# Attention with the keys on partitions: scores transposed, exp without a maximum, row sums by a product with ones

## The chip, the core and the metric

The kernel runs on one core of one Trainium2 chip. The metric is the device time of one execution in microseconds (us); the kernel before takes 4026.67 us, the median of 3 runs (4023.98 to 4026.76). All data are fp32.

## The reference

A block of an image network: group norm, attention over the 1024 pixels with 4 heads, a projection and a residual. `x` is [16, 512, 32, 32], so 16 batches of 512 channels by n = 1024 pixels.

```python
xg = x.reshape(b, NUM_GROUPS, -1)                       # 8 groups of 64 channels
mu = jnp.mean(xg, axis=-1, keepdims=True)
var = jnp.var(xg, axis=-1, keepdims=True)
xn = ((xg - mu) * jax.lax.rsqrt(var + EPS)).reshape(b, c, h, w)
xn = xn * norm_gamma[:, None, None] + norm_beta[:, None, None]
qkv = jnp.einsum('oc,bchw->bohw', qkv_w, xn) + qkv_b[:, None, None]
q, k, v = jnp.split(qkv, 3, axis=1)                     # each to [b, 4 heads, n, 128]
attn = jax.nn.softmax(jnp.einsum('bhnd,bhmd->bhnm', q, k) * scale, axis=-1)
out = jnp.einsum('bhnm,bhmd->bhnd', attn, v)
out = jnp.einsum('oc,bchw->bohw', proj_w, out) + proj_b[:, None, None]
return x + out
```

Inputs and weights are random normal, the weights scaled so that q and k have a variance of about one; gamma is ones, beta and all biases are zeros (the kernel does not use that).

## The kernel before

Everything is laid out with channels on the 128 partitions, in four chunks of a batch, and pixels along the free axis. A head has 128 channels. The main loop runs over **steps** `s`: 16 batches x 4 heads x 8 blocks of 128 queries = 512 steps.

A step has five parts. `scores(s)` (L208) multiplies a block of 128 queries with all 1024 keys of the head, two products of 512 columns into one tile of two PSUM banks, with queries on partitions and keys along the free axis. VectorE takes the row's maximum (L213), ScalarE (ACT) the exponential with the maximum as its bias and the row's sum as a by-product (L216). `weights` (L221, L222) takes the reciprocal of the 128 sums, one element per partition, and scales the block with it. `transposes` (L232) turns the block on TensorE (PE), 8 transposes of 128x128 into PSUM, and VectorE (L235) and ACT (L237) copy four of them each to SBUF. After every four steps `weighted_sum` (L247) multiplies the 512 turned queries with v, 8 products of 512 columns, and ACT adds v's bias (L253).

Beside the steps run **units**, products that later heads need. `qk_unit` (L163) makes half of q or k of the next head, 4 products of 512 columns; q goes out through VectorE (L169), k through ACT (L171). `v_unit` (L177, L182) makes v of all heads for one block of 128 keys. `proj_unit` (L187, L192) makes the projection of the batch before and adds bias and residual, and SyncE stores it. `plan_head` lays them on the eight steps of a head with `spread`; the statistics and the normalisation (L146) of the next batch lie on heads 2 and 3. All these units, the small products of the group norm and the outputs of `weighted_sum` share the PSUM pool `ps_a` of two buffers.

The order of work on each engine comes from the program's text and from the scheduler of the tile framework, which moves instructions by its own estimate of when they can start. Each engine then takes its instructions strictly in that order, waiting on semaphores of other engines. At the start, 48 products (L103) of the weights with beta make a bias for q, k and v, since beta is not added to the normalised input.

## Time and profile before

| | us |
|---|---|
| median of 3 runs | 4026.67 (4023.98 to 4026.76) |
| profiled execution, span | 4023.7 |
| TensorE busy | 3996.6 (99%) |
| VectorE (DVE) busy | 1716.4 (43%) |
| ScalarE (ACT) busy | 1150.7 (29%) |
| GpSimd (POOL) busy | 16.8 |

The span runs from the first to the last instruction of the profiled execution. In the rows, PE is TensorE's matmuls and PEld its weight loads. A row of a group names the line, the engine, the operation, output and inputs, the shape and the number of instructions; behind the bar stand the busy time, the mean of one in ns, and the idle time of the engine just before them with what ended it. A timeline row begins with start and length in us. The profile counts two records for each fp32 product, and one for each transpose. "L135 PE pv" is the second product of the group norm, and L177's `pv` is v.

### The profile page before, as it was taken

Reading aid. Unit: us, or ns where it says so; the run is one execution under the profiler, and the core shown is the slowest. Engines: PE = TensorE matmul, PEld = TensorE weight load, DVE = VectorE, ACT = ScalarE, POOL = GpSimd, SP = SyncE. Lnnn points to the kernel's source line nnn. Section 1 sums busy time; section 2 is a strip of 40 time slices with the busy share of each in tenths; the row PEclk is TensorE's granted clock in tenths of the full one; section 3 lists DMA queues with packets and bytes.
Section 4 is the critical chain, followed back from the end, with each engine's and each line's share of the span. In section 5 each row is a group of like instructions: output and inputs, shape, how many; then the busy total and the mean of one; then the engine's idle time right before and its main releaser. Section 6 shows DMA issues by size and latency. Waiting matters only on the chain.

```text
span 4023.7 us, 30686 instructions
## 1 busy us (share of the span) xinstructions
PE 3996.6 (99%) x12448; PEld 2009.3 (50%) x12448; DVE 1716.4 (43%) x2688; ACT 1150.7 (29%) x1921; POOL 16.8 (0%) x22
## 2 busy tenths in 40 slices
PE   7999999999999999999999999999999999999999
PEld 4544545445454454544545455454544545545454
DVE  2434434344343443434435344453434434345343
ACT  1332323323232232322323223232222322323222
POOL 0000000000000000000000000000000000000000
PEclk9999999999999999999999999999999999999999
DMA  2001000010100101001010010100001000010000
GB/s 84 0 1 42 1 29 14 0 42 1 34 8 0 42 0 42 0 1 42 0 42 0 3 40 1 42 0 11 32 1 42 1 17 26 0 42 1 11 11 21
DMA packets 29517, 73.28 MB, mean 18 GB/s; under 512 B 3776, under 2 KB 3776, under 8 KB 29376
## 3 DMA queue, kind: packets, MB, share of 16 engines
q1 hardware_dynamic: 27648, 67.12, 4.8%
q10 hardware_dynamic: 1728, 4.21, 0.3%
q8 instruction: 97, 1.59, 0.2%
q14 instruction: 44, 0.36, 0.0%
HBM read 37.76 MB, written 33.55 MB: 18 GB/s over the span
## 4 chain that ended last, share of the span: by engine, by line
PE 99%; DMA 0%; DVE 0%; ACTq 0%; issue 0%; POOL 0%; ACT 0%
PE pqk L163 22%; PE po L247 22%; PE s L208 22%; PE t L232 11%; PE pp L187 11%; PE pv L177 11%; PE pb L103 0%; DMA x<-in_x 0%; DMA wqkv<-in_qkv_wT 0%; PE pv L135 0%; PE pm L124 0%; ACTq L86 0%; DVE pt L235 0%; POOL rstd L139 0%; DVE xn L146 0%
## 5 line engine op out<-in xcount | busy, mean ns | idle before, releaser
L208 PE MATMUL s<-qk,qk 128*128 128x512 f32 x2048 | 965.9, 593 | 0.0
L163 PE MATMUL pqk<-xn,wqkv 128*128 128x512 f32 x2048 | 918.2, 594 | 2.4 <-DVE xn L146 2.4
L247 PE MATMUL po<-pt,v 128*128 128x512 f32 x2048 | 901.3, 593 | 0.3 <-DVE pt L235 0.3
L213 DVE TENSOR_REDUCE nmax<-s 128x1 f32<-128x1024 f32 x512 | 623.1, 1217 | 484.0 <-PE s L208 483.4
L235 DVE COPY pt<-t 128x512 f32<-128x512 f32 x512 | 351.3, 686 | 1052.5 <-PE t L232 1052.5
L216 ACT ACTIVATE p<-s,nmax 128x1024 f32<-128x1024 f32 x512 | 571.2, 1116 | 600.9 <-DVE nmax L213 600.7
L163 PEld LDWEIGHTS pqk<-xn,wqkv 128*128 128x128 f32 x2048 | 390.1, 191 | 493.5 <-issue 486.5
L247 PEld LDWEIGHTS po<-pt,v 128*128 128x128 f32 x2048 | 387.7, 190 | 482.6 <-issue 465.7
L232 PEld LDWEIGHTS t<-ident,p 128*128 128x128 f32 x4096 | 479.2, 141 | 264.3 <-issue 240.7
L232 PE MATMUL t<-ident,p 128*128 128x128 f32 x4096 | 531.7, 273 | 2.0 <-DVE p L222 1.3
L237 ACT COPY pt<-t 128x512 f32<-128x512 f32 x512 | 299.8, 586 | 639.0 <-PE t L232 638.6
L208 PEld LDWEIGHTS s<-qk,qk 128*128 128x128 f32 x2048 | 349.4, 190 | 246.2 <-issue 246.2
L177 PE MATMUL pv<-wqkv,xn 128*128 128x512 f32 x1024 | 449.4, 592 | 0.0
L187 PE MATMUL pp<-o,wproj 128*128 128x512 f32 x1024 | 449.4, 592 | 0.0
L222 DVE TENSOR_SCALAR p<-p,rinv 128x1024 f32<-128x1024 f32 x512 | 383.7, 749 | 10.1
L253 ACT ACTIVATE o<-po,bias 128x512 f32<-128x512 f32 x128 | 87.9, 687 | 952.4 <-PE po L247 952.4
L187 PEld LDWEIGHTS pp<-o,wproj 128*128 128x128 f32 x1024 | 194.6, 190 | 244.9 <-issue 239.4
L177 PEld LDWEIGHTS pv<-wqkv,xn 128*128 128x128 f32 x1024 | 194.6, 190 | 244.9 <-issue 230.6
L221 DVE RECIPROCAL rinv<-total 128x1 f32<-128x1 f32 x512 | 83.4, 163 | 398.5 <-ACT p L216 396.1
L171 ACT ACTIVATE qk<-pqk,bias 128x512 f32<-128x512 f32 x128 | 88.0, 687 | 374.7 <-PE pqk L163 374.7
L192 DVE SCALAR_TENSOR_TENSOR y<-pp,projb_sb,x 128x512 f32<-128x512 f32 x128 | 95.8, 749 | 165.0 <-PE pp L187 164.8
L182 ACT COPY v<-pv 128x512 f32<-128x512 f32 x128 | 74.9, 585 | 248.1 <-PE pv L177 248.1
(30 smaller groups left out, 443.6 us busy)
## 6 DMA issues: line engine op xcount, KB each, us to landing
x<-in_x SPq DMA_DIRECT2D x64, 512.0 KB, 3.6
out_y<-y SPq DMA_DIRECT2D x128, 256.0 KB, 2.2
wqkv<-in_qkv_wT ACTq DMA_DIRECT2D x4, 768.0 KB, 8.5
wproj<-in_proj_wT ACTq DMA_DIRECT2D x4, 256.0 KB, 8.2
gamma_sb<-in_gamma ACTq DMA_DIRECT2D x1, 2.0 KB, 3.8
beta_sb<-in_beta ACTq DMA_DIRECT2D x1, 2.0 KB, 4.7
qkvb_sb<-in_qkv_b ACTq DMA_DIRECT2D x1, 6.0 KB, 5.9
projb_sb<-in_proj_b ACTq DMA_DIRECT2D x1, 2.0 KB, 5.6
```

The lines of the kernel that those rows point to most:

```text
L163: nc.tensor.matmul(acc, wqkv[c][:, ts(o, P)], xns[b, c][:, ts(half, HALF)], start=(c == 0), stop=(c == NCC - 1),)
L177: nc.tensor.matmul(acc[:, :C], xns[b, c][:, ts(j, P)], wqkv[c][:, 2 * C : 3 * C], start=(c == 0), stop=(c == NCC - 1),)
L187: nc.tensor.matmul(acc, wproj[c][:, ts(o, P)], os_[b, c][:, ts(half, HALF)], start=(c == 0), stop=(c == NCC - 1),)
L192: nc.vector.scalar_tensor_tensor(y, acc, projb_sb[:, o : o + 1], xs[b, o][:, ts(half, HALF)], ALU.add, ALU.add)
L208: nc.tensor.matmul(sc[:, ts(half, HALF)], qs[b, h][:, ts(qb, P)], ks[b, h][:, ts(half, HALF)], start=True, stop=True,)
L213: nc.vector.tensor_reduce(nmax, sc, AX.X, ALU.max, negate=True)
L216: nc.scalar.activation(p, sc, AF.Exp, bias=nmax, accum_out=total)
L222: nc.vector.tensor_scalar_mul(ps[s], ps[s], rinv)
L232: nc.tensor.transpose(pt[:, i, :], p[:, ts(4 * g + i, P)], ident)
L235: nc.vector.tensor_copy(dst, pt)
L237: nc.scalar.copy(dst, pt)
L247: nc.tensor.matmul(acc, vs[b, j][:, ts(h, P)], pt[:, j, :], start=(j == 0), stop=(j == NB - 1),)
```

## The change

**Scores.** The operands of the products change places: the block of a step is now 128 keys on partitions, and the 1024 queries lie along the free axis. ACT takes the exponential straight from PSUM, with the factor 1/sqrt(128) as its scale, without a maximum and without the sum. The result has the keys on partitions, which is the form that the product with v needs: the maxima, `weights` and `transposes` with their copies are gone.

**Sums.** VectorE adds the eight blocks of a head into `tot` (L255, L257). At the head's end `denominators` multiplies `tot` with a matrix of ones (L264), two products of 512 columns in `ps_a`; each partition then has all sums. VectorE takes their reciprocals, 128x512 each (L266), and one instruction (L269) takes the larger of a sum and its reciprocal and adds these along the row into a column of `spans`.

**Output.** `weighted_sum` now follows each step: two products of 512 columns (L280) add into `po`, a tile of two PSUM banks that lives for a whole head, in a pool `ps_o` with one buffer. At the head's end VectorE multiplies it with the reciprocals (L288).

**Biases and beta.** The products with beta at the start are gone. Beta is added to the normalised input (L72), on VectorE for batch 0, on GpSimd for the others. The scale leaves q, and both q and k go out through ACT (L208). v's bias is added as v leaves PSUM, on VectorE (L221).

**General branch.** At the end the sums in `spans` are added and compared with 1e20. If they are larger or not a number, `flag` is 1, and the branch `general_path` does all batches again with the maximum, the sums and the transposes, in a loop over batches. It stands in the program, and each engine loads the flag and branches.

```diff
+    def apply(self, xn, x, mu, sc, c, eng):
+        self.nc.vector.tensor_scalar(
+            xn, x, mu[:, c : c + 1], sc[:, c : c + 1], ALU.subtract, ALU.mult
+        )
+        eng.tensor_scalar(xn, xn, self.beta[:, c : c + 1], None, ALU.add)
...
+    redo = nc.values_load(flag[0:1, 0:1], min_val=0, max_val=1,
...
+    with tc.If(redo > 0):
+        with ExitStack() as general:
+            general_path(
...
     ppool = ctx.enter_context(tc.tile_pool(name="p", bufs=4))
-    ptpool = ctx.enter_context(tc.tile_pool(name="pt", bufs=2))
+    lpool = ctx.enter_context(tc.tile_pool(name="l", bufs=2))
     ypool = ctx.enter_context(tc.tile_pool(name="y", bufs=3))
-    small = ctx.enter_context(tc.tile_pool(name="small", bufs=6))
     gn = ctx.enter_context(tc.tile_pool(name="gn", bufs=2))
     ps_s = ctx.enter_context(tc.tile_pool(name="ps_s", bufs=2, space=bass.MemoryType.PSUM))
-    ps_t = ctx.enter_context(tc.tile_pool(name="ps_t", bufs=2, space=bass.MemoryType.PSUM))
+    ps_o = ctx.enter_context(tc.tile_pool(name="ps_o", bufs=1, space=bass.MemoryType.PSUM))
     ps_a = ctx.enter_context(tc.tile_pool(name="ps_a", bufs=2, space=bass.MemoryType.PSUM))
...
-    # beta goes through the qkv product as a bias: W (xhat * gamma) + (W beta + b)
-    bias = const.tile([P, NOC], F32, name="bias")
-    for o in range(NOC):
-        pb = ps_a.tile([P, HALF], F32, tag="acc", name=f"pb_{o}")
-        for c in range(NCC):
-            nc.tensor.matmul(
-                pb[:, 0:1], wqkv[c][:, ts(o, P)], beta_sb[:, c : c + 1],
-                start=(c == 0), stop=(c == NCC - 1),
-            )
-        nc.vector.tensor_add(bias[:, o : o + 1], pb[:, 0:1], qkvb_sb[:, o : o + 1])
...
     def normalise(b, c):
-        xn = xnpool.tile([P, N], F32, tag="xn", name=f"xn_{b}_{c}")
-        nc.vector.tensor_scalar(
-            xn, xs[b, c], mus[b][:, c : c + 1], scs[b][:, c : c + 1],
-            ALU.subtract, ALU.mult,
-        )
-        xns[b, c] = xn
+        xns[b, c] = xnpool.tile([P, N], F32, tag="xn", name=f"xn_{b}_{c}")
+        norm.apply(xns[b, c], xs[b, c], *scaled[b], c, nc.vector if b == 0 else nc.gpsimd)
...
-        dst = store[b, h][:, ts(half, HALF)]
-        if which == 0:
-            nc.vector.tensor_scalar(dst, acc, bias[:, o : o + 1], SCALE, ALU.add, ALU.mult)
-        else:
-            nc.scalar.activation(dst, acc, AF.Identity, bias=bias[:, o : o + 1])
+        nc.scalar.activation(
+            store[b, h][:, ts(half, HALF)], acc, AF.Identity, bias=qkb_sb[:, o : o + 1]
+        )
...
         vs[b, j] = vpool.tile([P, C], F32, tag="v", name=f"v_{b}_{j}")
-        nc.scalar.copy(vs[b, j], acc[:, :C])
+        nc.vector.tensor_add(vs[b, j], acc[:, :C], vb_sb)
...
-    # ---- attention, one block of 128 queries of a head at a time ----
-    ps, sums, pts = {}, {}, {}
+    ps, tot, po, rinv = {}, {}, {}, {}
     def where(s):
-        bh, qb = divmod(s, NB)
-        return (*divmod(bh, HEADS), qb)
+        bh, j = divmod(s, NB)
+        return (*divmod(bh, HEADS), j)
     def scores(s):
-        b, h, qb = where(s)
+        b, h, j = where(s)
         sc = ps_s.tile([P, N], F32, tag="s", name=f"s_{s}")
         for half in range(NH2):
             nc.tensor.matmul(
-                sc[:, ts(half, HALF)], qs[b, h][:, ts(qb, P)], ks[b, h][:, ts(half, HALF)],
+                sc[:, ts(half, HALF)], ks[b, h][:, ts(j, P)], qs[b, h][:, ts(half, HALF)],
                 start=True, stop=True,
             )
-        nmax = small.tile([P, 1], F32, tag="nmax", name=f"nmax_{s}")
-        nc.vector.tensor_reduce(nmax, sc, AX.X, ALU.max, negate=True)
-        p = ppool.tile([P, N], F32, tag="p", name=f"p_{s}")
-        total = small.tile([P, 1], F32, tag="total", name=f"total_{s}")
-        nc.scalar.activation(p, sc, AF.Exp, bias=nmax, accum_out=total)
-        ps[s], sums[s] = p, total
-    def weights(s):
-        rinv = small.tile([P, 1], F32, tag="rinv", name=f"rinv_{s}")
-        nc.vector.reciprocal(rinv, sums.pop(s))
-        nc.vector.tensor_scalar_mul(ps[s], ps[s], rinv)
-    def transposes(s):
+        ps[s] = ppool.tile([P, N], F32, tag="p", name=f"p_{s}")
+        nc.scalar.activation(ps[s], sc, AF.Exp, scale=SCALE)
+        if j == 1:
+            tot[b, h] = lpool.tile([P, N], F32, tag="tot", name=f"tot_{b}_{h}")
+            nc.vector.tensor_add(tot[b, h], ps[s - 1], ps[s])
+        elif j > 1:
+            nc.vector.tensor_add(tot[b, h], tot[b, h], ps[s])
+    def denominators(b, h):
+        t = tot.pop((b, h))
+        for half in range(NH2):
+            l = ps_a.tile([P, HALF], F32, tag="acc", name=f"l_{b}_{h}_{half}")
+            nc.tensor.matmul(l, ones, t[:, ts(half, HALF)], start=True, stop=True)
+            r = lpool.tile([P, HALF], F32, tag=f"rinv{half}", name=f"rinv_{b}_{h}_{half}")
+            nc.vector.reciprocal(r, l)
+            worst = lpool.tile([P, HALF], F32, tag="worst", name=f"worst_{b}_{h}_{half}")
+            i = (b * HEADS + h) * NH2 + half
+            nc.vector.scalar_tensor_tensor(
+                worst, l, 1.0, r, ALU.mult, ALU.max, accum_out=spans[:, i : i + 1]
+            )
+            rinv[b, h, half] = r
+    def weighted_sum(s):
+        b, h, j = where(s)
         p = ps.pop(s)
-        chunk, qi = divmod(s, QPH)
-        if qi == 0:
-            pts[chunk] = ptpool.tile([P, NB, HALF], F32, tag="pt", name=f"pt_{chunk}")
-        for g in range(NB // 4):
-            pt = ps_t.tile([P, 4, P], F32, tag="t", name=f"t_{s}_{g}")
-            for i in range(4):
-                nc.tensor.transpose(pt[:, i, :], p[:, ts(4 * g + i, P)], ident)
-            dst = pts[chunk][:, 4 * g : 4 * g + 4, ts(qi, P)]
-            if g % 2 == 0:
-                nc.vector.tensor_copy(dst, pt)
-            else:
-                nc.scalar.copy(dst, pt)
-    def weighted_sum(chunk):
-        b, h, qb = where(chunk * QPH)
-        half = qb // QPH
-        pt = pts.pop(chunk)
-        if half == 0:
+        if j == 0:
+            po[b, h] = ps_o.tile([P, N], F32, tag="o", name=f"po_{b}_{h}")
+        for half in range(NH2):
+            nc.tensor.matmul(
+                po[b, h][:, ts(half, HALF)], vs[b, j][:, ts(h, P)], p[:, ts(half, HALF)],
+                start=(j == 0), stop=(j == NB - 1),
+            )
+        if j == NB - 1:
+            o = po.pop((b, h))
             os_[b, h] = opool.tile([P, N], F32, tag="o", name=f"o_{b}_{h}")
-        acc = ps_a.tile([P, HALF], F32, tag="acc", name=f"po_{chunk}")
-        for j in range(NB):
-            nc.tensor.matmul(
-                acc, vs[b, j][:, ts(h, P)], pt[:, j, :],
-                start=(j == 0), stop=(j == NB - 1),
-            )
-        # a row of the softmax sums to one, so v's bias is added to the sum
-        o = 2 * HEADS + h
-        nc.scalar.activation(
-            os_[b, h][:, ts(half, HALF)], acc, AF.Identity, bias=bias[:, o : o + 1]
-        )
+            for half in range(NH2):
+                nc.vector.tensor_mul(
+                    os_[b, h][:, ts(half, HALF)], o[:, ts(half, HALF)], rinv.pop((b, h, half))
+                )
...
-                spread(plan, proj_units(b - 1), 3, 7)
+                spread(plan, proj_units(b - 1), 2, 7)
...
     steps = B * HEADS * NB
     plan = []
-    for s in range(steps + 3):
+    for s in range(steps + 1):
         if s < steps:
-            b, h, qb = where(s)
-            if qb == 0:
+            b, h, j = where(s)
+            if j == 0:
                 plan = plan_head(b, h)
             scores(s)
-            for u in plan[qb]:
+            for u in plan[j]:
                 u()
-        if 1 <= s <= steps:
-            weights(s - 1)
-        if s >= 3 and (s - 3) % QPH == QPH - 1:
-            weighted_sum((s - 3) // QPH)
-        if 2 <= s < steps + 2:
-            transposes(s - 2)
+        if s > 0:
+            if s % NB == 0:
+                denominators(*where(s - 1)[:2])
+            weighted_sum(s - 1)
+    total = gn.tile([P, 1], F32, tag="total", name="total")
+    nc.vector.tensor_reduce(total, spans, AX.X, ALU.add)
+    fine = gn.tile([P, 1], F32, tag="fine", name="fine")
+    nc.vector.tensor_scalar(fine, total, LIMIT, None, ALU.is_le)
+    nc.vector.tensor_scalar(flag, fine, -1.0, 1.0, ALU.mult, ALU.add)
     for u in proj_units(B - 1):
         u()
```

The change also moves instructions. On TensorE, where a head (here the third of batch 0) follows another, these rows stood before; `t` are the transposes, `s` the scores, `pqk` a unit:

```order
L208 MATMUL s_754<-qk_0_1_427,qk_0_1_348 128x512 x2
L232 MATMUL t_0_765<-ident,p_695 128x128 x4
L232 MATMUL t_1_771<-ident,p_695 128x128 x4
L208 MATMUL s_777<-qk_0_2_668,qk_0_2_552 128x512 x2
L163 MATMUL pqk_3_0_0_786<-xn_0_250,wqkv_124 128x512
L163 MATMUL pqk_3_0_0_786<-xn_1_252,wqkv_126 128x512
L163 MATMUL pqk_3_0_0_786<-xn_2_254,wqkv_128 128x512
L163 MATMUL pqk_3_0_0_786<-xn_3_256,wqkv_130 128x512
L232 MATMUL t_0_795<-ident,p_718 128x128 x4
L232 MATMUL t_1_801<-ident,p_718 128x128 x4
```

Nothing ties the two heads together there. At the same place of the changed kernel, behind the unit `pqk_3_0_0`, TensorE has these; `l` are the sums, `po_1` is the old head's output and `po_2` the new head's:

```order
L264 MATMUL l_1_0_484<-tot_1_400,ones 128x512
L264 MATMUL l_1_1_490<-tot_1_400,ones 128x512
L280 MATMUL po_1_402<-p_467,v_7_267 128x512 x2
L247 MATMUL s_501<-qk_0_2_371,qk_0_2_433 128x512 x2
L247 MATMUL s_511<-qk_0_2_371,qk_0_2_433 128x512 x2
L247 MATMUL s_530<-qk_0_2_371,qk_0_2_433 128x512 x2
L204 MATMUL pqk_3_0_1_517<-xn_0_175,wqkv_66 128x512
L204 MATMUL pqk_3_0_1_517<-xn_1_178,wqkv_67 128x512
L280 MATMUL po_2_508<-p_475,v_0_218 128x512 x2
```

Three score tiles and half a unit now lie between the sums and the new head's first output product `po_2`, which waits for VectorE. VectorE has at that place:

```order
L257 TENSOR_TENSOR tot_1_400<-tot_1_400,p_467 128x1024
L266 RECIPROCAL rinv_1_0_486<-l_1_0_484 128x512
L266 RECIPROCAL rinv_1_1_492<-l_1_1_490 128x512
L269 SCALAR_TENSOR_TENSOR worst_1_0_488,spans<-l_1_0_484,rinv_1_0_486 128x512
L269 SCALAR_TENSOR_TENSOR worst_1_1_494,spans<-l_1_1_490,rinv_1_1_492 128x512
L288 TENSOR_TENSOR o_1_498<-po_1_402,rinv_1_0_486 128x512
L288 TENSOR_TENSOR o_1_498<-po_1_402,rinv_1_1_492 128x512
L255 TENSOR_TENSOR tot_2_506<-p_475,p_504 128x1024
```

The two products that empty `po_1` (L288) stand behind both reciprocals and both L269. From head 2 to head 3 of a batch the last `tot` addition stands behind the next batch's four normalisations:

```order
L64 TENSOR_TENSOR sc<-rstd,gamma_sb 128x4
L69 TENSOR_SCALAR xn_0_620<-x_0_356,mu,sc 128x1024
L69 TENSOR_SCALAR xn_1_623<-x_1_358,mu,sc 128x1024
L69 TENSOR_SCALAR xn_2_650<-x_2_360,mu,sc 128x1024
L69 TENSOR_SCALAR xn_3_653<-x_3_362,mu,sc 128x1024
L257 TENSOR_TENSOR tot_2_506<-tot_2_506,p_610 128x1024
L266 RECIPROCAL rinv_2_0_628<-l_2_0_626 128x512
```

In the program's text the normalisations belong to head 3; here they have moved ahead of the end of head 2's sum.

More of the change, by code (lines that the diff above doesn't have):

```diff
@@ L6 @@
 from concourse import mybir
-from concourse.bass import ts
+from concourse.bass import ds, ts
 from concourse.masks import make_identity
@@ L14 @@
 AX = mybir.AxisListType
+P = 128
 HEADS = 4
@@ L70, in attention_block @@
     load_x(0)
-    ident = const.tile([P, P], F32, name="ident")
-    make_identity(nc, ident)
-    avg = const.tile([P, P], F32, name="avg")
     nc.vector.memset(avg, 0.0)
@@ L114, in stats_chunk @@
             mvs[b] = gn.tile([P, NCC, 2], F32, tag="mv", name=f"mv_{b}")
[L115 to L118 removed]
+        norm.chunk(mvs[b], xs[b, c], c)
     def stats_group(b):
[L121 to L150 removed]
+        scaled[b] = norm.group(mvs.pop(b))
+    def normalise(b, c):
+        xns[b, c] = xnpool.tile([P, N], F32, tag="xn", name=f"xn_{b}_{c}")
+        norm.apply(xns[b, c], xs[b, c], *scaled[b], c, nc.vector if b == 0 else nc.gpsimd)
     def qk_unit(b, h, which, half):
```

211 lines of the change are left out of this document (162 added, 49 removed).

## Prediction

> **What bounds the kernel now.** I read the page first: the busy table, the slices and the chain of waits.
>
> ```profile
> span 4023.7 us, 30686 instructions
> PE 3996.6 (99%) x12448; PEld 2009.3 (50%) x12448; DVE 1716.4 (43%) x2688; ACT 1150.7 (29%) x1921; POOL 16.8 (0%) x22
> PE   7999999999999999999999999999999999999999
> PEclk9999999999999999999999999999999999999999
> PE pqk L163 22%; PE po L247 22%; PE s L208 22%; PE t L232 11%; PE pp L187 11%; PE pv L177 11%; PE pb L103 0%; DMA x<-in_x 0%; DMA wqkv<-in_qkv_wT 0%; PE pv L135 0%; PE pm L124 0%; ACTq L86 0%; DVE pt L235 0%; POOL rstd L139 0%; DVE xn L146 0%
> ```
>
> TensorE works in every slice but the first, at the full granted clock, and 99% of the chain is its own matmuls. DVE and ACT are under half full. So a matmul taken away is worth its whole slot, and anything that makes TensorE wait costs its whole length. A busy time cannot price a slot, since matmuls overlap (the transposes' 531.7 us would be 13% of the span; the chain gives them 11%). The slots come from the starts in the timeline of TensorE, in the middle of the run:
>
> ```profile
> 1007.66 1.04 PE L232 MATMUL t<-ident,p 128*128 128x128 f32 x8
> 1008.53 1.88 PE L208 MATMUL s<-qk,qk 128*128 128x512 f32 x4
> 1010.25 7.03 PE L177 MATMUL pv<-wqkv,xn 128*128 128x512 f32 x16
> 1017.12 1.04 PE L232 MATMUL t<-ident,p 128*128 128x128 f32 x8
> ```
>
> Eight transposes take 1008.53 - 1007.66 = 0.87 us (0.109 each); 16 records of 512 columns take 1017.12 - 1010.25 = 6.87 us (0.429 each). The profile counts two records per fp32 product, so a product is 0.86 us, and a `scores` or a pair of `po` products is 1.72.
>
> **Removed and added on TensorE.** The groups by line:
>
> ```profile
> L232 PE MATMUL t<-ident,p 128*128 128x128 f32 x4096 | 531.7, 273 | 2.0 <-DVE p L222 1.3 <-ACT pt L237 0.7
> L103 PE MATMUL pb<-beta_sb,wqkv 128*128 128x1 f32 x96 | 21.3, 353 | 17.6 <-DMA wqkv<-in_qkv_wT 16.4 <-DVE bias L107 1.2
> ```
>
> All 4096 transposes go: 4096 x 0.1087 = -445 us. The products with `ones` are 2 per head, 64 heads, 128 products: 128 x 0.859 = +110 us. `scores` only swaps its operands, and `weighted_sum` has the same 1024 products, so both keep their slots.
>
> **The start.** The chain of waits up to the first qk product, and VectorE's timeline there:
>
> ```profile
> 21.62 17.23 PE pb L103 x80
> 43.12 16.81 PE pqk L163 x32
> 13.78 0.17 DVE L122 COPY mean<-mv 128x4 f32<-128x4 f32 x1
> 20.82 0.69 DVE L117 BATCH_NORM_STATS2 st<-x 128x6 f32<-128x512 f32 x1 [0.72 <-DMA x<-in_x]
> 42.26 2.98 DVE L146 TENSOR_SCALAR xn<-x,mu,sc 128x1024 f32<-128x1024 f32 x4
> ```
>
> Batch 0's means stand at 13.78, then the pb products hold the group statistics back. In the new order the statistics matmuls come first, and what is left ahead of the first qk product is the wait for batch 1's third chunk (20.82), two bn_stats of 0.68, `sc` 0.2, two normalisations and one beta addition (0.75 each): 20.82 + 1.4 + 0.2 + 2.3 + gaps 0.2 = 24.9 instead of 43.1, so -18.2 us.
>
> **What is hidden.** Durations come from these groups:
>
> ```profile
> L216 ACT ACTIVATE p<-s,nmax 128x1024 f32<-128x1024 f32 x512 | 571.2, 1116 | 600.9 <-DVE nmax L213 600.7 <-ACT pt L237 0.2
> L213 DVE TENSOR_REDUCE nmax<-s 128x1 f32<-128x1024 f32 x512 | 623.1, 1217 | 484.0 <-PE s L208 483.4
> L235 DVE COPY pt<-t 128x512 f32<-128x512 f32 x512 | 351.3, 686 | 1052.5 <-PE t L232 1052.5
> L192 DVE SCALAR_TENSOR_TENSOR y<-pp,projb_sb,x 128x512 f32<-128x512 f32 x128 | 95.8, 749 | 165.0 <-PE pp L187 164.8
> L146 DVE TENSOR_SCALAR xn<-x,mu,sc 128x1024 f32<-128x1024 f32 x64 | 47.7, 809 | 0.6
> L171 ACT ACTIVATE qk<-pqk,bias 128x512 f32<-128x512 f32 x128 | 88.0, 687 | 374.7 <-PE pqk L163 374.7
> ```
>
> The leanest step is a `scores` and a `po` pair, 3.44 us of TensorE. In it ACT has one exp (1.12) and VectorE one addition to `tot`: by L192 at 512 columns plus L213 less L235 for 512 more, 0.75 + 0.53 = 1.28. Both fit under the 1.72 us of the products between the score tile and its use. Without that cover each would cost its length 512 and 448 times. The evictions that change engines (q to ACT 0.69, v to VectorE 0.75, o to VectorE) hide the same way. VectorE in all: 448 x 1.28, 128 reciprocals, 128 each of L269, L288, v and y at 0.75, and the norm, about 1500 us, no bound.
>
> **The head boundary.** Here TensorE can really wait. The output accumulator `po` has one buffer of two banks, and the next head's first `po` product waits until both L288 products have read it. Ahead of these VectorE runs two reciprocals and two L269, in the order shown above. Count from the end of the first `l` product, with R for a reciprocal of 128x512, 0.05 us for a semaphore, 0.16 for the sum that L269 also writes (the one-element row below), and between VectorE instructions 0.04, as from 1003.71 to 1003.75 here:
>
> ```profile
> 1003.55 0.16 DVE L221 RECIPROCAL rinv<-total 128x1 f32<-128x1 f32 x1 [1.33 <-ACT p L216]
> 1003.75 0.75 DVE L222 TENSOR_SCALAR p<-p,rinv 128x1024 f32<-128x1024 f32 x1
> ```
>
>  VectorE releases `po` at 0.05 + 2R + 4 x 0.75 + 2 x 0.16 + 5 x 0.04 + 0.05 = 2R + 3.62. TensorE meanwhile has the second `l` (0.86), the old head's last `po` (1.72), three score tiles (5.16) and half a unit (1.72): 9.46 us. The half unit needs the PSUM buffer of `l`, free at 2R + 1.09; that is late only when 2R + 1.09 > 7.74, and the time of `po` above is later in any case. So **the wait per head is 2R - 5.84 us**, if positive: none up to R = 2.92.
>
> R has no row at this size. The rows with one to four elements are:
>
> ```profile
> L221 DVE RECIPROCAL rinv<-total 128x1 f32<-128x1 f32 x512 | 83.4, 163 | 398.5 <-ACT p L216 396.1
> L107 DVE TENSOR_TENSOR bias<-pb,qkvb_sb 128x1 f32<-128x1 f32 x12 | 1.8, 156 | 13.6 <-PE pb L103 13.6
> L131 DVE TENSOR_TENSOR d<-d 128x4 f32<-128x4 f32 x16 | 2.6, 163 | 0.6
> L129 DVE TENSOR_TENSOR d<-mean,mu 128x4 f32<-128x4 f32 x16 | 2.6, 162 | 0.6
> L133 DVE TENSOR_TENSOR vv<-d,mv 128x4 f32<-128x4 f32 x16 | 2.4, 153 | 0.0
> ```
>
> One element of reciprocal stands above a plain instruction by 7 ns (L107), 3 (L131, less 3 ns for its three further elements at L213's 1.04), 4 (L129 likewise) or 13 (L133 likewise). The median is 5.5 ns per element and the mean 6.75; I take 6: R = 512 x 6 + 160 = 3.23 us. The lower bound is a plain streaming instruction, 0.75 us; the upper is 13 ns, 6.82 us. At 3.23 the wait is 0.62 us, in 63 heads 39 us.
>
> [...]
>
> **Head 2 to 3, and GpSimd.** Here no qk unit covers VectorE, which runs `sc`, four normalisations and the last `tot` addition before `l` may start: 1.3 + 0.2 + 4 x 0.81 + 1.28 = 6.0 us after the second statistics product, against 6.0 us of products on TensorE (half a `po` pair 0.86, three groups of 1.72). GpSimd's additions of beta (1024 columns, now in 15 batches) are needed 7.7 us after `l`. Their price has no row; from the two at 128 columns
>
> ```profile
> masks.py:199 POOL TENSOR_SCALAR_AFFINE_SELECT ident<-ident 128x128 f32<-128x128 f32 x1 | 0.3, 292 | 0.1
> masks.py:197 POOL MEMSET ident<- 128x128 f32 x1 | 0.2, 205 | 0.3 <-POOLq L349 0.3
> ```
>
> eight times gives 1.6 to 2.3 us each, four of them 6.6 to 9.3, starting as the normalisations end; mostly covered. I take 0; the other end is the fourth rival.
>
> **The end.** In the last head no score tiles follow. The projection waits for a PSUM buffer until 2R + 1.09 = 7.6 after `l` instead of 2.6, and 5.0 us late; the boundary into that head has no half unit as cover, +1.7; with the last `o` product's own wait about +8 us. Each engine then loads `flag` and branches; no row shows that. I take 3 us, between nothing and the landing time of two transfers as small as these, one to load and one for the code behind the branch:
>
> ```profile
> out_y<-y SPq DMA_DIRECT2D x128, 256.0 KB, 2.2
> gamma_sb<-in_gamma ACTq DMA_DIRECT2D x1, 2.0 KB, 3.8
> ```
>
> **Sum**, in the profiled execution: from the first qk product to the end of the last product stand
>
> ```profile
> 43.10:4020.00 3976.90, 3974.34 (x12348) 1987.47 (x12348) 1700.02 (x2639) 1149.43 (x1920) 15.11 (x15) 1.00 0.05 16
> 4019.82 0.75 DVE y L192
> ```
>
> 4019.8 - 43.1 = 3976.7. Then 24.9 + 3976.7 - 445 + 110 + 3.9 (as now from the last product to the end) + 8 + 3 = 3681.5, without boundary waits; + 39 = 3720.5. The median of the runs lies 3.0 above the profiled span: **3724 us**, 7.5% faster.
>
> **Rivals.** (1) *The reciprocal costs more*: R from 3.74 (7 ns) to 5.3 (10 ns). The one row with exactly one element says 7, which speaks for it; L131 and L129 speak against. At 4.5 the wait is 3.16 us and the time 3684.5 + 63 x 3.16 = 3884; the ends are 3788 and 3984. [...] (2) *It streams*, or the cover is enough: no wait, 3684. The 163 ns beside L131's 163 speak for it. (3) *Slower than before*: the wait eats the whole gain. The gain without waits is 4026.7 - 3684.5 = 342 us, 5.43 us per head; it is gone from R = 5.64 us, 10.7 ns per element. Only L133 allows that; its 13 ns give 3684.5 + 63 x 7.8 = 4176. (4) *GpSimd and VectorE hinder each other* in the normalisation: three additions of beta ahead of VectorE's last steps, 3 x 1.6 x 15 batches = +72, 3796. Against it: VectorE's next instruction starts 0.04 us after its last, while GpSimd began 0.09 after its release (ve ends 40.91, rstd starts 41.00):
>
> ```profile
> 40.75 0.16 DVE L137 TENSOR_SCALAR ve<-pv 128x4 f32<-128x4 f32 x1 [0.69 <-PE pv L135]
> 41.00 1.02 POOL L139 TENSOR_TENSOR rstd<-ve,neghalf 128x4 f32<-128x4 f32 x1 [39.70 <-DVE ve L137]
> ```
>
> [...] (5) *The general branch runs*: the old method once more behind the new, over 7000 us. A row's sum of 1024 exponentials of scores of about unit variance is some 1700, far below 1e20.
>
> **Chances.** Forecast 0.52 (its own range 3684 to 3790), (1) 0.22, (2) 0.08, (3) 0.03, (4) 0.13, (5) 0.01, others 0.01. The range 3672 to 3885 holds the forecast, (2), (4) and over half of (1). About 0.2% is what a measurement of this kernel can tell; only (3), (5) and the tail of others are not faster: 0.95 faster, 0.01 same, 0.04 slower.
>
> **What would show it.** No L232; L264 x256 at 0.43; first qk product near 25 us; TensorE 98% busy; a wait of the first `po` of a head on VectorE's L288 of some 0.6 us, 63 times, and R near 3.2 us at L266. Wrong would be: R above 3.7, waits of `l` on `tot` at every fourth head, waits of `s` on exp, or a lower clock after the waits.

## The result and the profile after

The changed kernel takes 3696.05 us (3695.53 to 3696.66, 4 runs) beside 4025.59 for the kernel before (4023.98 to 4026.76, 4 runs): a ratio of 0.9182, interval 0.9169 to 0.9195, 8.2% faster. The forecast was 3724. The page of the profiled execution:

```profile
span 3694.5 us, 20904 instructions
PE 3654.3 (99%) x8512; PEld 1608.1 (44%) x8512; DVE 1470.9 (40%) x1596; ACT 701.1 (19%) x769; POOL 200.2 (5%) x80
PE   7999999999999999999999999999999999999998
```

TensorE is again busy in every slice, with 8512 matmul records instead of 12448. The 4096 transposes and the 96 records of pb are gone, 256 records of `l` have come: 12448 - 4096 - 96 + 256 = 8512. The old method behind the flag did not run. The groups on which the forecast's terms rested:

```profile
L257 DVE TENSOR_TENSOR tot<-tot,p 128x1024 f32<-128x1024 f32 x384 | 470.2, 1225 | 1233.0 <-ACT p L252 1219.1
L247 PE MATMUL s<-qk,qk 128*128 128x512 f32 x2048 | 941.6, 592 | 0.0
L252 ACT ACTIVATE p<-s 128x1024 f32<-128x1024 f32 x512 | 523.9, 1023 | 1949.5 <-PE s L247 1947.1
L266 DVE RECIPROCAL rinv<-l 128x512 f32<-128x512 f32 x128 | 420.4, 3326 | 301.3 <-PE l L264 301.3
L264 PE MATMUL l<-tot,ones 128*128 128x512 f32 x256 | 130.7, 618 | 6.1 <-DVE tot L257 6.1
L280 PE MATMUL po<-p,v 128*128 128x512 f32 x2048 | 961.6, 593 | 0.0
L226 PE MATMUL pp<-o,wproj 128*128 128x512 f32 x1024 | 457.3, 595 | 5.5 <-DVE worst L269 5.5
L72 POOL TENSOR_SCALAR xn<-xn,beta_sb 128x1024 f32<-128x1024 f32 x60 | 183.5, 3072 | 19.0 <-DVE xn L69 16.1
L69 DVE TENSOR_SCALAR xn<-x,mu,sc 128x1024 f32<-128x1024 f32 x64 | 59.8, 994 | 0.5
```

The number behind the second bar is the idle time ahead of the group, with what ended it. `po` (L280) shows 0.0: the wait at the head boundary, the forecast's largest uncertain term, isn't there. `l` waited 6.1 us in all and the projection once, 5.5 us. The reciprocal takes 3.326 us, an addition of beta on GpSimd 3.07 us.

### The profile page after: what moved, and what is told of

Its sections match the earlier page's. It is cut to its first block, busy times and chain, and to the rows that moved or that the text cites. A ratio compares the mean times of both kernels' runs of the same rounds, so it can differ in the third digit from the quotient of the medians.

```text
span 3694.5 us, 20904 instructions
## 1 busy us (share of the span) xinstructions
PE 3654.3 (99%) x8512; PEld 1608.1 (44%) x8512; DVE 1470.9 (40%) x1596; ACT 701.1 (19%) x769; POOL 200.2 (5%) x80
## 4 chain that ended last, share of the span: by engine, by line
PE 92%; DVE 2%; POOL 0%; issue 0%; POOLq 0%
PE pqk L204 22%; PE po L280 22%; PE s L247 21%; PE pp L226 12%; PE pv L216 11%; PE l L264 3%; DVE xn L69 2%; DVE tot L257 0%; POOL rstd L62 0%; DVE rinv L266 0%; PE pv L58 0%; DVE sc L64 0%; DVE ve L60 0%; PE pm L47 0%; DVE y L231 0%
## 5 line engine op out<-in xcount | busy, mean ns | idle before, releaser
L280 PE MATMUL po<-p,v 128*128 128x512 f32 x2048 | 961.6, 593 | 0.0
L257 DVE TENSOR_TENSOR tot<-tot,p 128x1024 f32<-128x1024 f32 x384 | 470.2, 1225 | 1233.0 <-ACT p L252 1219.1
L252 ACT ACTIVATE p<-s 128x1024 f32<-128x1024 f32 x512 | 523.9, 1023 | 1949.5 <-PE s L247 1947.1
L280 PEld LDWEIGHTS po<-p,v 128*128 128x128 f32 x2048 | 386.8, 190 | 475.5 <-issue 456.1
L266 DVE RECIPROCAL rinv<-l 128x512 f32<-128x512 f32 x128 | 420.4, 3326 | 301.3 <-PE l L264 301.3
L208 ACT ACTIVATE qk<-pqk,qkb_sb 128x512 f32<-128x512 f32 x256 | 175.9, 687 | 978.6 <-PE pqk L204 978.6
L221 DVE TENSOR_TENSOR v<-pv,vb_sb 128x512 f32<-128x512 f32 x128 | 88.5, 691 | 266.7 <-PE pv L216 266.7
L72 POOL TENSOR_SCALAR xn<-xn,beta_sb 128x1024 f32<-128x1024 f32 x60 | 183.5, 3072 | 19.0 <-DVE xn L69 16.1
L38 DVE BATCH_NORM_STATS2 st<-x 128x6 f32<-128x512 f32 x128 | 82.3, 683 | 143.4 <-DMA x<-in_x 143.4
L264 PE MATMUL l<-tot,ones 128*128 128x512 f32 x256 | 130.7, 618 | 6.1 <-DVE tot L257 6.1
L288 DVE TENSOR_TENSOR o<-po,rinv 128x512 f32<-128x512 f32 x128 | 82.1, 683 | 0.0
L255 DVE TENSOR_TENSOR tot<-p,p 128x1024 f32<-128x1024 f32 x64 | 77.8, 1216 | 7.2 <-ACT p L252 7.2
```

The costliest lines, as they stand in the source:

```text
L72: eng.tensor_scalar(xn, xn, self.beta[:, c : c + 1], None, ALU.add)
L208: nc.scalar.activation(store[b, h][:, ts(half, HALF)], acc, AF.Identity, bias=qkb_sb[:, o : o + 1])
L252: nc.scalar.activation(ps[s], sc, AF.Exp, scale=SCALE)
L257: nc.vector.tensor_add(tot[b, h], tot[b, h], ps[s])
L264: nc.tensor.matmul(l, ones, t[:, ts(half, HALF)], start=True, stop=True)
L266: nc.vector.reciprocal(r, l)
```

## Experiments

The first eight runs answer four questions: what the removed and the added products are worth, what the boundary costs without its cover, what the guard and GpSimd cost, and whether the small waits can be removed. The last three follow up what these showed. A time without a range is that of a single run.

### The slots: no transposes, no products with ones, no pb products

In the kernel before, `po` reads the blocks of `p` as they lie, and the evictions of the transposes become copies of the same size:

```diff
-            for i in range(4):
-                nc.tensor.transpose(pt[:, i, :], p[:, ts(4 * g + i, P)], ident)
...
-                nc.vector.tensor_copy(dst, pt)
+                nc.vector.tensor_copy(dst, pv[:, g])
```

> The kernel before, with the 4096 transposes left out; the copies of L235 and L237 read the untransposed block from SBUF instead of PSUM, so the output is not the reference's. Theory (each transpose is worth its slot of 0.109 us): 445 us less, 3581 us. Rival (part of the slots only fills waits for VectorE and ACT, which then come out): 3700 us or more.

Measured: 3586.44 us, 438 below the kernel before, timed beside it (4024.7). The forecast's term was -445. Part of the 7 us between them are waits that this run has and the kernel before has not: `po` waits 4.1 us once, `s` 1.8 us.

In the changed kernel, the products with `ones` are left out and the reciprocal reads `tot`:

```diff
-            nc.tensor.matmul(l, ones, t[:, ts(half, HALF)], start=True, stop=True)
```

> The changed kernel without the products with ones: the reciprocals read tot itself, so the output is not the reference's. Theory (128 products at 0.86 us, plus the waits of 0.18 and 0.53 us before them): 110 + 9 = 119 us less, 3577 us, if the reciprocals stay covered without the sums' own slots; up to 3640 if from head 2 to 3 the cover is now too short. Rival (the sums' slots only fill a wait for VectorE): 3690.

Measured: 3582.25 us, 114 below the changed kernel. The term was +110. That the two are so close is partly chance. The waits ahead of `l` (6.1 us) go with the products, and of the 5.5 us at the end 2.2 are left; in their place a new wait has come at the 15 boundaries from head 2 to 3:

```profile
PE pqk L204 <- POOL xn L72: 15.6, 15, 1.1
```

Without the sums' own slots TensorE reaches the next batch's unit before GpSimd has added beta.

In the kernel before, the products of beta with the weights go out of the start:

```diff
-        for c in range(NCC):
-            nc.tensor.matmul(
-                pb[:, 0:1], wqkv[c][:, ts(o, P)], beta_sb[:, c : c + 1],
...
+    nc.vector.tensor_copy(bias, qkvb_sb)
```

> The kernel before, with the products of the weights with beta at the start left out (beta is zero here, so the bias is the qkv bias alone). Theory: the group statistics of batch 0 are no longer held back, the first qk product starts near 25 instead of 43 us and the whole takes 18 us less, 4007.5. Rival (the weights' transfers hold the start): under 5 us less.

Measured: 4005.66 us (4005.44 to 4005.99), ratio 0.9953, interval 0.9936 to 0.9970, 19 us less. TensorE's timeline at the start, first of this run, then of the changed kernel:

```profile
22.68 7.50 PE L156 MATMUL pqk<-xn,wqkv 128*128 128x512 f32 x12 [3.10 <-DVE xn L139]
```

```profile
24.48 16.33 PE L204 MATMUL pqk<-xn,wqkv 128*128 128x512 f32 x32 [4.27 <-DVE xn L72]
```

The first qk product starts at 22.68 and 24.48 instead of 43.12. So pb held the start. The changed kernel gives 1.8 us of it back, but not for the additions of beta (L72) alone: the run below without them starts at 24.17, with two small instructions and one more of the statistics ahead of its first normalisation.

What follows: three large terms (-445, +110, -18.2) hold, each within some 7 us, though the runs that take something out also move some waits. The rest of the forecast's error has to lie in the waits.

### The boundary with less cover

A score tile may not be issued before the output product of two steps earlier, so that one score tile instead of three stands between the old head's sums and the new head's `po`:

```diff
+        with tc.issue_after(last[s - 2].ins) if s > 1 else ExitStack():
...
-            nc.tensor.matmul(
+            last[s] = nc.tensor.matmul(
                 po[b, h][:, ts(half, HALF)], vs[b, j][:, ts(h, P)], p[:, ts(half, HALF)],
```

> The changed kernel with one edge more: a score tile may not be issued before the output product of two steps earlier, so that the three score tiles ahead of the new head's first output product shrink to one. Theory (the reciprocals are hidden only by the products that stand between the sums and the new head's first output product): the PSUM buffer for the next unit comes free about 7.4 us after the first sum (two reciprocals of 3.29, one L269), TensorE has 0.86 + 1.72 + 1.72 = 4.30 us until then and waits 3.1 us at each of 63 boundaries: 3696 + 195 = 3891 us. Rival (VectorE is only 40% busy, so the order does not matter): 3696 us, no wait.

Measured: 3974.07 us, 278 above the changed kernel, more than either side expected. The timeline of TensorE at one boundary, and the table by stretches (us, busy times of PE, PEld, DVE, ACT and POOL, granted clock, DMA share, GB/s) behind the wait:

```profile
288.51 1.88 PE L248 MATMUL s<-qk,qk 128*128 128x512 f32 x4
293.12 4.32 PE L226 MATMUL pp<-o,wproj 128*128 128x512 f32 x6 [2.73 <-DVE worst L270]
297.29 1.88 PE L281 MATMUL po<-p,v 128*128 128x512 f32 x4
```

```profile
293.12:297.30 4.18, 4.18 (x7) 1.91 (x8) 2.89 (x5) 0.00 (x0) 0.00 (x0) 0.64 0.02 4
297.30:302.00 4.70, 4.70 (x12) 2.08 (x11) 0.22 (x1) 1.02 (x1) 0.00 (x0) 1.00 0.00 0
```

The wait is where the expectation had it: TensorE does not wait for `po` but for the PSUM buffer of `l`, which L269 (L270 here) reads last. The clock was not in it: behind the 2.73 us of idling the granted clock is 0.64 over 4.18 us, and six records take 297.29 - 293.12 = 4.17 us instead of 6 x 0.43 = 2.58, 1.6 us more. The waits of the whole run (us in total, times, longest):

```profile
PE pqk L204 <- DVE worst L270: 87.6, 32, 2.7
PE pp L226 <- DVE worst L270: 46.5, 16, 5.5
PE pqk L204 <- POOL xn L72: 45.2, 15, 3.0
```

Without the one of 5.5 us, which stands at the end of the changed kernel too, these are 62 waits of 173.8 us in all: 47 for L269, and 15, from head 2 to 3, put down to GpSimd's additions. The clock is not lower behind all of them. Behind one of the longest it stays at 1.00:

```profile
952.85 2.81 PE L204 MATMUL pqk<-xn,wqkv 128*128 128x512 f32 x6 [3.02 <-POOL xn L72]
952.85:957.00 4.15, 4.15 (x10) 1.97 (x11) 2.79 (x5) 0.00 (x0) 0.00 (x0) 1.00 0.02 4
```

Behind the waits of 2.73 us at 293.12 and 368.18 it is 0.64, over 4.18 and 4.22 us; what tells these from the wait of 3.02 us was not shown. The mean granted clock is 0.977 over the 3972.2 us of this run and 0.999 over the 3694.5 of the changed kernel, so 91 us of clock are missing here and 4 there: by that some 87 us are lost. A wait is counted from the modelled end of the last record, 0.59 us behind its start, while the slot is 0.43: 62 x 0.16 = 10 us more. In the last batch `po` waits 4.8 us once. Together some 276 of the 278; the last digit of the mean clock is worth 4 us.

The other way round, each reciprocal runs twice, and the order is left to the scheduler, which now puts five score tiles ahead of the next unit:

```diff
             nc.vector.reciprocal(r, l)
+            nc.vector.reciprocal(r, l)
```

> The changed kernel with each reciprocal of a head taken twice, 6.6 us more of VectorE per head. The scheduler now puts five score tiles ahead of the new head's unit. Theory (boundary with a cover that the scheduler sizes): buffer free 14.0 us after the first sum, cover 0.86 + 1.72 + 8.6 = 11.2, so 2.8 us of wait per head, 3696 + 63 x 2.8 = 3872 us, less than half of the added 418 us. Rival 1 (reciprocals lie wholly on the path): 3696 + 418 = 4114. Rival 2 (wholly hidden): 3696.

Measured: 3961.92 us, +266, 90 more than the theory said. The same two views:

```profile
286.71 8.75 PE L247 MATMUL s<-qk,qk 128*128 128x512 f32 x20
297.75 4.54 PE L226 MATMUL pp<-o,wproj 128*128 128x512 f32 x6 [2.29 <-DVE worst L270]
```

```profile
297.75:302.13 4.38, 4.38 (x7) 1.82 (x8) 4.17 (x7) 0.00 (x0) 0.00 (x0) 0.61 0.00 0
```

A wait of 2.29 us, again for L269, and 4.38 - 2.58 = 1.8 us for the clock. The 62 waits of this run come to 146 us. The mean granted clock is 0.974 over 3960.0 us, so by the same working some 99 us are lost. The slots add 10 as above, the end's wait grows from 5.5 to 11.9 us, and `po` waits 4.3 us once in the last batch: some 266, beside 266 measured, with the same uncertainty of the clock. So what the reciprocals add is paid at the boundary, less the score tiles that move there.

Two later runs test these two readings. First, one score tile as cover as above, with L269 left out, so that the buffer of `l` is free when its reciprocal ends:

```diff
-            nc.vector.scalar_tensor_tensor(
-                worst, l, 1.0, r, ALU.mult, ALU.max, accum_out=spans[:, i : i + 1]
-            )
```

> The run with the score tiles in order (one score tile as cover, 3974.1 us) once more, with L269 (the comparison that keeps worst and spans) left out and spans set to 1. In that run TensorE waited 2.73 us at every head for L269 of the first half: the half unit needs the PSUM buffer of l, which L269 reads last, behind both reciprocals. Theory (the buffer of l is what is waited for, not po): without L269 the buffer is free when the first reciprocal ends, about 3.4 us after its l product, and TensorE needs it 4.3 us after; po is released 2 x 3.3 + 2 x 0.64 = 7.9 us after, and needed 4.3 + 3 x 0.86 = 6.9 after at the earliest: a wait of about 1.0 us or less. Without a loss of clock that is 3690 + 63 x 1.0 = 3753 or less. Rival (po is what holds, with all of its release time): waits of 2 us and more and a lower clock behind them, 3690 + 63 x 3.6 = 3917.

Measured: 3705.88 us. The same boundary:

```profile
275.52 1.88 PE L249 MATMUL s<-qk,qk 128*128 128x512 f32 x4
277.24 4.46 PE L227 MATMUL pp<-o,wproj 128*128 128x512 f32 x10
281.53 1.88 PE L277 MATMUL po<-p,v 128*128 128x512 f32 x4
```

No wait is left here, and `po` does not wait either. It was the buffer of `l`. The run still takes 16 us more than the one without L269 and with three score tiles (3689.96, below): the 15 boundaries from head 2 to 3 keep a wait of 0.4 us for GpSimd's additions, and `po` waits 3.6 us once in the last batch, 9 us in all; the rest is not told apart.

Second, with L269, two score tiles as cover:

```diff
-        with tc.issue_after(last[s - 2].ins) if s > 1 else ExitStack():
+        with tc.issue_after(last[s - 3].ins) if s > 2 else ExitStack():
```

> The same order as in the run with the score tiles in order, but a score tile may now run ahead of the output product of three steps earlier, so that two score tiles cover the head boundary instead of one (the changed kernel has three). Theory A (cover is time, and a short wait costs only itself): the wait falls from 2.73 us by one score tile, 1.72, to 1.0 us, and TensorE keeps its clock: 3696 + 63 x 1.0 = 3759. Theory B (every wait of this kind also lowers the granted clock and costs 1.6 us more, as 2.73 did): 3696 + 63 x 2.6 = 3860. Theory C (the boundary was covered by something else than score tiles): 3696.

Measured: 3784.18 us, +88.

```profile
277.25 3.60 PE L248 MATMUL s<-qk,qk 128*128 128x512 f32 x8
281.87 2.84 PE L226 MATMUL pp<-o,wproj 128*128 128x512 f32 x6 [1.02 <-DVE worst L270]
284.54 1.88 PE L281 MATMUL po<-p,v 128*128 128x512 f32 x4
```

```profile
281.87:286.00 4.13, 4.13 (x10) 1.98 (x11) 4.03 (x6) 0.04 (x1) 0.00 (x0) 1.00 0.01 4
```

The wait is one score tile shorter, 1.02 us, and the clock stays at 1.00: 284.54 - 281.87 = 2.67 us for six records. This is theory A in kind. Its sum of 63 us is too small: the waits of these boundaries and of GpSimd's additions (15 of 1.3) come to some 67 us, the slots behind them to 62 x 0.16 = 10, the slower first records (2.67 us for six instead of 2.58) to 6, and a wait of `po` in the last batch to 3; the 2 us that are left lie within what the mean clock, 0.998 beside 0.999, leaves open.

What follows: in the changed kernel the boundary is covered by its three score tiles. From the end of the last score tile's slot, TensorE waits 281.87 - (277.25 + 3.43) = 1.2 us with two tiles and 293.12 - (288.51 + 1.72) = 2.9 us with one: the first tile fewer costs its 1.72 us less the margin that three tiles leave, the next one all of its 1.72, and where the clock behind the wait is 0.64 or 0.61, as above, 1.6 to 1.8 us come on top.

### The guard

The guard is L269, the comparison that feeds the flag of the general branch. It is left out of the changed kernel (the same edit, `spans` set to 1).

> The changed kernel without L269, which writes the test values of the general branch (the test then reads ones). 1.3 us less of VectorE per head. Theory (hidden by the products between): only the end gains, since the projection's PSUM buffer comes free one instruction earlier and after one reciprocal instead of two: 3696 - 6 = 3690 us. Rival (VectorE's chain at the boundary is still on the path): 63 x 1.3 = 82 us less, 3614.

Measured: 3689.96 us (3689.79 to 3690.96), 6 below the changed kernel; ratio to before 0.9169, interval 0.9155 to 0.9183. The wait ahead of the last projection falls from 5.5 to 2.1 us in two parts, and the clock behind it stays at 1.00. The guard costs TensorE what it adds at the end, where nothing covers it. At the 63 other boundaries it is free, as long as the cover stands.

### GpSimd's additions

Beta is folded into the normalisation, `x * sc + (beta - mu * sc)`, so that VectorE does it in one pass and GpSimd adds nothing:

```diff
-            xn, x, mu[:, c : c + 1], sc[:, c : c + 1], ALU.subtract, ALU.mult
+            xn, x, sc[:, c : c + 1], mu[:, c : c + 1], ALU.mult, ALU.add
         )
-        eng.tensor_scalar(xn, xn, self.beta[:, c : c + 1], None, ALU.add)
```

> The changed kernel with beta folded into the normalisation: one VectorE instruction x * sc + (beta - mu * sc) per chunk, two small instructions of four columns more per batch, and GpSimd without its 60 additions of 3.07 us. Theory (the wait of the sums on tot from head 2 to 3 comes from GpSimd's hold on VectorE's normalisations): the mean of L69 goes from 0.99 back to 0.75-0.81 us, the wait of 0.53 us goes, 15 x 0.63 = 9.5 us less and 1 us at the start: 3685.5. Rival (the normalisations' own length makes the wait): under 3 us less.

Measured: 3688.98 us (3688.18 to 3690.50), 7.1 less than the changed kernel; ratio to before 0.9165, interval 0.9153 to 0.9178. The normalisation's line in the changed kernel and then in this run (minimum/median/maximum in ns):

```profile
L69 DVE TENSOR_SCALAR xn<-x,mu,sc x64: 796/808/1609, 22.2 to 3392.7; 128x1024 f32<-128x1024 f32 x64
```

```profile
L73 DVE TENSOR_SCALAR xn<-x,sc,nb x64: 796/808/814, 23.3 to 3387.3; 128x1024 f32<-128x1024 f32 x64
```

Without GpSimd's additions none of the 64 normalisations takes more than 0.814 us; beside them one of the four took 1.6 in each of the 15 batches. So the two engines do hinder each other. But VectorE is not held for GpSimd's whole instruction: the normalisation loses 0.8 us, beside an addition of 3.7 us that starts 0.44 us before it (in one of the 15 batches 3.3 us and 0.1 us). The row of the waits of `l` for `tot`, 6.1 us in the changed kernel, is gone in this run, which is most of the 7.1; the first qk product starts only 0.3 us earlier, at 24.17.

### The rest of the waits, and a faster kernel

On top of the folded beta: the sums are issued ahead of the units (so that the second `l` does not wait for the eviction of a unit), the last head's sums use score buffers, and batch 1's statistics wait until batch 0 is normalised.

```diff
+        with tc.issue_after(scaled[0, NCC - 1].ins) if b == 1 else ExitStack():
+            norm.chunk(mvs[b], xs[b, c], c)
...
+            if b == B - 1 and h == HEADS - 1:
+                l = ps_s.tile([P, N], F32, tag="s", name=f"l_{b}_{h}_{half}")[:, :HALF]
...
+        if s > 0 and s % NB == 0:
+            denominators(*where(s - 1)[:2])
+        if s < steps:
             for u in plan[j]:
                 u()
```

> As the kernel with the one-pass normalisation, and three moves: the sums of a head before the unit of that step (so they do not wait for ACT to empty a unit's PSUM buffer, 48 x 0.18 us), the last head's sums in the score tiles' PSUM (so the projection finds its buffers free), and batch 1's statistics behind batch 0's normalisation. Theory: -8.6, -8 (5.5 of wait and most of the slow clock after it) and -6 from 3685.5: 3663 us. Rival (the waits come back elsewhere): 3680 or more.

Measured: 3669.23 us (3668.45 to 3670.14), ratio to before 0.9117, interval 0.9105 to 0.9130: 26.8 less than the changed kernel, where 33 were expected. The three moves have no runs of their own; what each gives is read from this run's rows. Its start and its end:

```profile
18.66 11.83 PE L208 MATMUL pqk<-xn,wqkv 128*128 128x512 f32 x23 [2.78 <-DVE xn L73]
3631.14 1.02 PE L287 MATMUL po<-p,v 128*128 128x512 f32 x2
3638.88 22.84 PE L230 MATMUL pp<-o,wproj 128*128 128x512 f32 x52 [1.56 <-DVE o L295]
```

The first qk product is 24.48 - 18.66 = 5.8 us earlier. From the last `po` to the end of the projection it takes 3661.7 - 3631.1 = 30.6 us, where the changed kernel takes 3689.2 - 3652.1 = 37.1:

```profile
3652.08 1.02 PE L280 MATMUL po<-p,v 128*128 128x512 f32 x2
3658.60 30.60 PE L226 MATMUL pp<-o,wproj 128*128 128x512 f32 x64 [5.50 <-DVE worst L269]
```

The waits of `l` for ACT (below) have no row in this run. With 7.1 for GpSimd and some 8.6 for the second `l` these make 5.8 + 6.5 + 7.1 + 8.6 = 28.0 against 26.8 measured.

Last, the product with `ones` runs on a bf16 copy of the sums:

```diff
-    ones = const.tile([P, P], F32, name="ones")
+    ones = const.tile([P, P], BF16, name="ones")
...
+        elif j == NB - 1:
+            t = lpool.tile([P, N], BF16, tag="tot16", name=f"tot16_{b}_{h}")
+            nc.vector.tensor_add(t, tot[b, h], ps[s])
+            tot[b, h] = t
```

> The fastest version so far (beta folded into the normalisation, denominators ahead of the units, the two ends shortened: 3669.2 us) with one more edit: the last addition to tot writes a bf16 tile, ones is bf16, and the 128 products with ones run on these. The changed part of the computation is that the partial sums are rounded to bf16 before they are summed over the partitions. Theory (a product taken out of TensorE's queue gives back its whole slot, as the run without these products showed with 114 us): a bf16 product takes one record instead of two. By the rows a record of 512 columns has a slot of 0.43 us at most, so at least 128 x 0.43 = 55 us less: 3614 or below. [...] Rival: the shorter products are less cover at the head boundary and for the l buffers, and a wait appears instead: above 3640.

Measured: 3587.08 us (3585.69 to 3588.38), ratio to before 0.8909, interval 0.8893 to 0.8925, 82.2 less than the version above. The products with `ones` have 128 records in the whole run instead of 256, and the two of a head take 257.65 - 257.22 = 0.43 us, 0.215 each:

```profile
257.22 0.59 PE L276 MATMUL l<-tot,ones 128*128 128x512 bf16 x2
257.65 1.88 PE L292 MATMUL po<-p,v 128*128 128x512 f32 x4
```

So a bf16 product of 512 columns takes one record instead of two, and its slot is a quarter of the fp32 product's 0.859 us, where the bound of 3614 took a half: 128 x 0.644 = 82 us, as measured. It is the fastest kernel here. The version at 3669 us is the fastest that keeps everything in fp32.

## Why the prediction was right, and where it was not

**Transposes, products with ones, start.** -445, +110 and -18.2 were right; the runs gave -438, +114 and -19 (this last on the kernel before). The first two of these hold some waits beside the slots, as said above.

**Hidden work.** Right: `s` and `po` have no idle time ahead of them, with exp at 1.02 us (1.12 taken) and the addition to `tot` at 1.22 (1.28 taken).

**The head boundary: this is the step that failed.** R was right: 3.326 us, 3.23 taken, though with some luck, since the rows gave anything from 3 to 13 ns per element and 6 was picked among them. The wait that was worked out from R, 0.62 us per head and 39 in all, isn't there. The mis-sized term is what stands behind the reciprocals. VectorE and TensorE at a boundary of the changed kernel:

```profile
197.81 6.57 DVE L266 RECIPROCAL rinv<-l 128x512 f32<-128x512 f32 x2 [1.22 <-PE l L264]
204.30 0.63 DVE L269 SCALAR_TENSOR_TENSOR worst<-l,rinv 128x512 f32<-128x512 f32 x1
204.85 0.08 DVE L269 DVE_READ_ACCUMULATOR worst<-l,rinv 128x1 f32 x1
205.47 1.28 DVE L288 TENSOR_TENSOR o<-po,rinv 128x512 f32<-128x512 f32 x2
```

```profile
196.65 1.99 PE L264 MATMUL l<-tot,ones 128*128 128x512 f32 x4 [0.37 <-DVE tot L257]
200.19 5.31 PE L247 MATMUL s<-qk,qk 128*128 128x512 f32 x12
205.34 1.88 PE L204 MATMUL pqk<-xn,wqkv 128*128 128x512 f32 x4
207.06 1.88 PE L280 MATMUL po<-p,v 128*128 128x512 f32 x4
```

The forecast gave the two L269, the two L288 and the gaps between them 3.52 us beside the semaphores (4 x 0.75 + 2 x 0.16 + 5 x 0.04). They take 206.75 - 204.30 = 2.45, since L269 and L288 last 0.6 to 0.7 and not 0.75, the accumulator's read 0.08 and not 0.16, and each starts before its predecessor's end instead of 0.04 behind it. So VectorE is done 8.94 us after the first reciprocal starts, where 2R + 3.52 with the measured R is 10.17. That is 1.2 us less, of which 0.25 go back, since the first reciprocal starts 1.16 us after the first `l` product and not 0.86 + 0.05. So the wait of 2 x 3.326 - 5.84 = 0.81 that the formula gives turns into a margin: L288 ends at 206.75, `po` starts at 207.06. 0.3 us decide here, from head 2 to 3; at 47 of the 63 boundaries it is 0.5. The cover of three score tiles and half a unit was right, and the runs with less of it show what it is worth. That `po` is released later than the buffer of `l` was right too; but with less cover the buffer of `l` is needed first, and becomes the wait.

**Head 2 to 3, GpSimd.** Taken as 0, it costs 7 (beta folded). GpSimd's addition takes 3.07 us and not 1.6 to 2.3, and stretches the normalisations. Four additions end 0.4 us before TensorE needs them, at 204.95 for 205.34:

```profile
191.68 3.78 DVE L69 TENSOR_SCALAR xn<-x,mu,sc 128x1024 f32<-128x1024 f32 x4
192.68 12.27 POOL L72 TENSOR_SCALAR xn<-xn,beta_sb 128x1024 f32<-128x1024 f32 x4 [1.22 <-issue]
```

The fourth rival's mechanism is there, at a tenth of its 72 us. It stretches the four normalisations by 3.78 - 2.98 = 0.8 us, not by three whole additions.

**Not in the forecast.** At the other boundaries the second `l` waits for ACT to empty its buffer, the last unit's. The row of the waits, and TensorE's timeline at one such place:

```profile
PEld l L264 <- ACT qk L208: 35.1, 47, 0.7
```

```profile
1026.49 2.07 PE L264 MATMUL l<-tot,ones 128*128 128x512 f32 x4
1028.40 1.88 PE L280 MATMUL po<-p,v 128*128 128x512 f32 x4
```

Most of that wait of the weight load lies beside the first `l`; what is left is 1028.40 - 1026.49 = 1.91 us for two products instead of 1.72, between 0.18 and 0.19 us, 47 times, 8.6 us.

**The end.** +8 was forecast, of waits alone. It is 5.5 us of waiting, and then the last projection takes 30.6 us instead of 64 x 0.43 = 27.5, since the granted clock is 0.90 there:

```profile
3658.00:3690.00 32.00, 30.60 (x64) 13.17 (x64) 8.86 (x17) 0.00 (x0) 0.00 (x0) 0.90 0.15 59
```

8.6 us, nearly the forecast's number, but a third of it for a reason that the forecast did not have. From the last product to the end of the span it is 5.3 us, where 6.9 were taken.

**The sum.** The forecast without boundary waits was 3681.5. With 8.6 for the second `l`, 7 for GpSimd, +0.6 and -1.6 at the end and -0.4 at the start it is 3695.7; the span is 3694.5. The median lies 1.6 above the span (3.0 taken). So the 28 us of error are the 39 of the wait that did not come, less the 14 of these five terms, with the 1.4 of the median and 1.2 that the sum leaves over. That the forecast is 28 us off and not more is in part luck: 14 us that it did not foresee stand against the 39 that did not come.

**Rivals.** At the boundary it came out as the second rival said, by its second reason: the cover is enough, though the reciprocal doesn't stream. The first and the third needed R from 3.74 and 5.64. Of the signs that would have shown the forecast wrong, two were there: `l` waits for `tot` at every fourth head, 15 times, and the clock is lower behind the one long wait, at the end. And of the signs that would have borne it out, the wait of a head's first `po` for L288 was missing.

## What to carry to other kernels

Where one engine sets the time, a removed instruction is worth its slot, read from starts and not from busy times, and these sums held within 5% (-438 for -445, +114 for +110, -19 for -18.2). A wait is a difference of two long chains: here 1.2 us of small overestimates on VectorE, in a chain of eight instructions, decided between 39 us and nothing, so such a wait deserves a range around its own sign. Cover is worth its own length here (the wait grew from 1.2 to 2.9 us with the next score tile of 1.72 gone) and can be lost by the order alone, and where a wait appeared, the buffer that is needed first decided, not the one that comes free last.

## What the hardware showed that was not expected

**Behind some waits the clock is lower, and the length of the wait does not tell which.** In the changed kernel the one wait of 5.5 us lasts until 3658.60, and the granted clock is 0.50 in 6.8 us around and behind its end:

```profile
3657.60:3664.40 6.80, 5.80 (x7) 2.53 (x8) 3.25 (x10) 0.00 (x0) 0.00 (x0) 0.50 0.00 1
```

With one score tile as cover it is 0.64 over 4.18 us behind a wait of 2.73 us, which costs 1.6 us more, and with each reciprocal twice 0.61 over 4.38 us behind 2.29 us, which costs 1.8. It stays at 1.00 behind a wait of 3.02 us in the first of these two runs, and behind the 1.02 us with two score tiles as cover. What decides between them was not shown.

**A reciprocal costs 6.2 ns per element** at 128x512 (3.326 us less the 0.16 of a one-element instruction, by 512).

**GpSimd is slow at a plain addition**: 3.07 us for 1024 columns, four times VectorE's 0.745 for the same operation (L72 on VectorE in batch 0):

```profile
L72 DVE TENSOR_SCALAR xn<-xn,beta_sb x4: 745/745/746, 23.7 to 27.1; 128x1024 f32<-128x1024 f32 x4
```
